# First layer: the loads of later weights and vector rows are asked for over steps 0 to 7 instead of all in step 0

## The chip, the cores and the metric

The kernel runs on one core of one Trainium2 chip. The metric is the device time of one execution in microseconds, the median of several runs. The kernel before takes 1694.06 us (three runs: 1685.83, 1694.06 and 1694.51).

## What is computed

Four layers follow each other on x, 64 sequences of 64 tokens with 128 features, with a context of the same shape. All is float32. The change lies in the first layer, an attention with relative positions and 16 heads of 64:

```python
kv = jnp.concatenate([memory, layer_input], axis=1)        # 128 keys for 64 queries
q = (layer_input @ Wq).reshape(b, q_len, n_head, d_head)
k = (kv @ Wk).reshape(b, kl, n_head, d_head)
v = (kv @ Wv).reshape(b, kl, n_head, d_head)
r = (pe @ Wr).reshape(kl, n_head, d_head)
ac = jnp.einsum('bqhd,bkhd->bhqk', q + content_bias, k)
bd = rel_shift(jnp.einsum('bqhd,khd->bhqk', q + position_bias, r))
scores = (ac + bd) * (1.0 / np.sqrt(d_head))
scores = jnp.where(slf_attn_mask[:, None, :, :], jnp.float32(-1000000000.0), scores)
attn = jax.nn.softmax(scores, axis=-1)
ctx = jnp.einsum('bhqk,bkhd->bqhd', attn, v).reshape(b, q_len, n_head * d_head)
out = layer_norm(layer_input + ctx @ Wo, ln1_g, ln1_b)
h = jax.nn.relu(out @ W1 + b1)
out = layer_norm(out + (h @ W2 + b2), ln2_g, ln2_b)
```

The second layer is self and cross attention with a feed-forward part, the third a gated fusion with the context, the fourth again two attentions and a choice of two among eight experts for each token.

## The kernel before

The 4096 tokens are cut into eight groups of eight sequences (512 tokens). In the first layer the sixteen heads are taken in eight pairs, so that there are 64 units, one for each group and pair of heads. `first_layer` runs them as a software pipeline that is written out by hand: one loop over steps t from -5 to 63 (line 605), in which each step holds work of several units. With `order["on"]` (line 1422) every engine keeps the order in which the first layer's instructions are written; the other layers are ordered by a scheduler when the program is built.

What a step t does, in the order of the code:

- `weights_turned` (line 536): the softmax weights of unit t are transposed on PE (`pt<-ident,s` in the profile) and copied out by DVE.
- `soft` (line 501): the scores of unit t+2 on PE (`psc`); DVE adds the relative part `skew` and takes the negated maximum `nm`; ACT takes eight exponentials (`s<-s,nm`).
- `keys` (line 468): the keys of unit t+3 on PE (`psk`), copied out by ACT as `kT`.
- `products` (line 547): weights times values of unit t (`av`), copied out by DVE.
- `values` (line 481): values for unit t+2 (`psv`), copied out half by ACT, half by DVE.
- `rel` (line 427): for unit t+5 the queries on PE (`proj<-kv,wq`), which DVE and ACT copy out as `qp` and `qc`; then the relative part (`pbd`), which DVE and ACT copy into `stage`. The shift of the relative part is made by way of DRAM: SP writes `stage` to `scr`, and when that has landed reads it back in two halves as `skew`.
- The output projection of unit t is added to `acc` on PE.
- `masked` (line 462): POOL adds the mask to a `skew` that was read back two steps before or so (`skew<-skew,mb`). `divided`: DVE takes the reciprocals of the sums `sm`, POOL multiplies.

In the steps -1, 7, 15 and so on SP loads the inputs of the next group (`kv`, 512 KB, and its mask, 64 KB) ahead of its `scr`. PSUM tiles of all these products come from one pool of seven banks (line 106). Transfers are issued by SP and ACT only here, each in the order of its queue; on ACT they stand among its arithmetic instructions.

The loads that the change touches stand in `later`, called at the end of step 0 (line 646), all on ACT's queue: `rows`, 22 vectors of 128 and one of 8, spread to all 128 partitions (a tile of 128x2824, 1412 KB); the feed-forward weights `w1_0` and `w2_0` of the first layer (256 KB each; `w` in the profile); `bd_small` and `wo1` (24 and 128 KB; `bd_small` and `wo`), from which `block_diagonal` makes weights of the second layer from step 12 on. The first five vectors of `rows` are those of the first layer and are read by `close` (line 563), which finishes a group and begins at the end of that group's last step, the first at step 7; the others are read by later layers. `later` also fills `pad` on POOL. From step 3 on each step sends a piece of `pad`, 325 KB, on ACT's queue to the DRAM buffer `hrows` (`empty_rows`, line 257), for the experts of the last layer.

Of the kernel before, what the change touches and what calls it, by code (L numbers as in the profile page):

```python
# [16 lines left out]
P = 128  # L17
B = 64
S = 64
D = 128  # L20
# [38 lines left out]
NROW = _RB + NE  # L59
# [35 lines left out]
def kernel(ctx: ExitStack, tc: tile.TileContext, a: dict, out: bass.AP):  # L95
    order = {"on": False}
    nc = Ordered(tc, order)
# [11 lines left out]
    def ctile(shape, name, dtype=F32):  # L109
        return const.tile(shape, dtype, tag=name, name=name)  # L110

    def wtile(shape, tag, bufs, dtype=F32):
        if tag in COMMON:
            return pools["common"].tile(shape, dtype, tag=tag, bufs=COMMON[tag], name=tag)
        return pools["work"].tile(shape, dtype, tag=tag, bufs=bufs, name=tag)
# [79 lines left out]
    rows = ctile([P, NROW], "rows")  # L195
# [10 lines left out]
    bd_small = ctile([P, 6, 8], "bd_small")  # L206
    qk1 = ctile([P, 2, D], "qk1")
    wo1 = ctile([P, 2, D], "wo1")
# [161 lines left out]
    def first_layer():  # L370
# [6 lines left out]
        w1_0 = wtile([P, 512], "w1", 1)  # L377
        w2_0 = wtile([P, NFC, D], "w2", 1)
# [34 lines left out]
        def mask_bias(g):  # L413
            nc.gpsimd.tensor_scalar(groups[g]["maskb"], groups[g]["m8"], NEG, None, ALU.mult)
# [5 lines left out]
        for h in range(2):  # L420
            pr = pmm("pr")
            for k in range(4):
                ks = slice(k * P, (k + 1) * P)
# [38 lines left out]
        def masked(sk, maskb):  # L462
            for r in range(2):
                nc.gpsimd.tensor_tensor(
                    sk[:, 4 * r : 4 * r + 4, :], sk[:, 4 * r : 4 * r + 4, :], maskb, ALU.add
                )

        def keys(p, kv):
            kT = wtile([P, NB, P], "kT0", 3)
            for hb in range(2):  # L470
                hs = slice(4 * hb, 4 * hb + 4)
                psk = pmm("psk")
                nc.tensor.matmul(
                    psk, lhsT=wk0[:, p * P : (p + 1) * P],
                    rhs=kv[:, hs, :, :].rearrange("p b c i -> p (b c i)"),
                    start=True, stop=True,
                )
                nc.scalar.copy(kT[:, hs, :], v3(psk[:, :], 4))
            return kT
# [21 lines left out]
        def soft(qc, kT, sk):  # L501
            psc2 = [pmm("psc") for _ in range(2)]
            for b in range(NB):
                for r in range(2):
                    rp = slice(64 * r, 64 * r + 64)
                    bp = slice(64 * (b % 2), 64 * (b % 2) + 64)
                    nc.tensor.matmul(
                        psc2[r][bp, (b // 2) * P : (b // 2 + 1) * P],
                        lhsT=qc[rp, b * S : (b + 1) * S],
                        rhs=kT[rp, b, :],  # L510
                        start=True,
                        stop=True,
                    )
            out = []
            for r in range(2):
                s = wtile([P, NBLK, P], "s", 6)
                nm = wtile([P, NBLK], "nm", 6)
                sm = wtile([P, NBLK], "sm", 6)
                nc.vector.tensor_tensor(s, v3(psc2[r][:, :], 4), sk[:, 4 * r : 4 * r + 4, :], ALU.add)
                nc.vector.tensor_reduce(nm, s, axis=AX.X, op=ALU.max, negate=True)  # L520
                for k in range(NBLK):
                    nc.scalar.activation(
                        s[:, k, :], s[:, k, :], AF.Exp,
                        bias=nm[:, k : k + 1], accum_out=sm[:, k : k + 1],
                    )
                out.append((s, sm))
            return out

        def divided(out):
            for s, sm in out:  # L530
                nc.vector.reciprocal(sm, sm)
            for s, sm in out:
                nc.gpsimd.tensor_tensor(s, s, last(sm[:, :], P), ALU.mult)
            return [s for s, sm in out]

        def weights_turned(ss):
            pTs = []
            for r in range(2):
                pt = pmm("pt0")
                for k in range(NBLK):  # L540
                    nc.tensor.transpose(pt[:, k * P : (k + 1) * P], ss[r][:, k, :], ident)
                pT = wtile([P, T], "pT", 4)
                nc.vector.tensor_copy(pT, pt)
                pTs.append(pT)
            return pTs

        def products(pTs, v, odd):
            av = pmm("av0")
            for b in range(NB):
                for r in range(2):  # L550
                    rp = slice(64 * r, 64 * r + 64)
                    nc.tensor.matmul(
                        av[rp, b * S : (b + 1) * S],
                        lhsT=v[:, b, odd, rp],
                        rhs=pTs[r][:, b * S : (b + 1) * S],
                        start=True,
                        stop=True,
                    )
            cx = wtile([P, T], "cx", 2)
            nc.vector.tensor_copy(cx, av)  # L560
            return cx
# [22 lines left out]

        pad = wtile([P, PADS, ROWW], "pad", 1)

        def later():
            nc.scalar.dma_start(rows, a["rows"].to_broadcast([P, NROW]))
            nc.scalar.dma_start(w1_0, a["w1_0"])
            nc.scalar.dma_start(w2_0, a["w2_0"].rearrange("(f c) d -> c f d", c=P))  # L590
            nc.scalar.dma_start(bd_small, a["bd"])
            nc.scalar.dma_start(wo1, a["wo1"])
            padi = wtile([P, PADS], "padi", 1, I32)
            nc.gpsimd.iota(padi, pattern=[[0, PADS]], base=2 * B * S, channel_multiplier=1)
            nc.gpsimd.memset(pad, 0.0)
            nc.gpsimd.tensor_copy(pad[:, :, D : D + 1].rearrange("p k c -> p (k c)"), padi)
            nc.gpsimd.memset(pad[:, :, D + 1 : D + 2], -1.0)
# [7 lines left out]
        for t in range(-REL, n):  # L605
            live = t >= 0
            if live:
                pTs = weights_turned(held[t]["s"])
            if 0 <= t + SOFT < n:
                h = held[t + SOFT]  # L610
                h["s"] = soft(h["qc"], h["k"], h["sk"])
            if 0 <= t + KEY < n:
                g, p = divmod(t + KEY, NP)
                held[t + KEY]["k"] = keys(p, groups[g]["kv"])
            if live:
                cx = products(pTs, vs[t // 2], t % 2)
            if 0 <= t + VAL < n:
                k = (t + VAL) // 2
                g, p = divmod(2 * k, NP)
                if t % 2 == 0:  # L620
                    vs[k] = wtile([P, NB, 2, P], "v0", 2)
                values(p, groups[g]["kv"], vs[k], t % 2)
            if t + REL < n:
                g, p = divmod(t + REL, NP)
                if p == 4 and g + 1 < NG:
                    load(g + 1)
                if p == 7 and g + 1 < NG:
                    mask_bias(g + 1)
                front = rel(p, groups[g])
                next(front)  # L630
            if live:
                g, p = divmod(t, NP)
                if p == 0:
                    acc = pools["psa"].tile([P, T], F32, tag="acc", name="acc")
                nc.tensor.matmul(acc, lhsT=wo0[:, p, :], rhs=cx, start=(p == 0), stop=(p == NP - 1))
                del held[t]
            if len(fresh) == 2 or t + REL >= n and fresh:
                masked(*fresh.pop(0))
            if 0 <= t + SOFT < n:
                held[t + SOFT]["s"] = divided(h["s"])  # L640
            if t + REL < n:
                qc, sk, maskb = next(front)
                held[t + REL] = {"qc": qc, "sk": sk}
                fresh.append((sk, maskb))
            if t == 0:
                later()
            if t == 12:
                folds = block_diagonal()
            if t >= 12:
                next(folds, None)  # L650
            if t > 2:
                empty_rows(t - 3, pad)
            if t > n - 12:
                empty_rows(t + 8, pad)
            if t == -REL:
                mask_bias(0)
            for e in list(ends):
                if next(e[1], "end") == "end":
                    ends.remove(e)
            if live and p == NP - 1:  # L660
                zT = wtile([P, T], "o", 2)
                nc.vector.tensor_tensor(
                    v3(zT[:, :], NB), v3(acc[:, :], NB), groups[g]["kv"][:, :, 1, :], ALU.add
                )
                ends.append((g, close(g, zT)))
# [860 lines left out]
```

## Time and profile before

| what | value |
|---|---|
| median of three runs | 1694.06 us |
| the profiled execution, on the device | 1692.51 us |
| its span in the profile | 1690.5 us |
| busy: PE, DVE, ACT, POOL | 92%, 69%, 59%, 53% |
| mean granted clock of PE | 0.943 |
| DMA packets' bytes over the span | 136.74 MB, mean 81 GB/s |
| queue of SP (q1), queue of ACT (q10) | 90.99 MB, 34.40 MB |
| `rows` load | one transfer, 1412 KB, issued at 50.1 us |

In the profile every instruction of the kernel has the line L74, that of the helper that records it, so groups are told apart by their tiles (`out<-in`). PE is TensorE's matmul row, PEld its weight loads; ACTq and SPq are the issuing of transfers on those two queues. In a timeline each row has the start, the time taken, the engine, the operation with its tiles, the count of merged instructions, and in brackets how long the engine had been idle before and what ended that. In a table of windows each engine has its busy time and, in brackets, its instructions; after them stand the clock that was granted to PE, the mean busy share of the 16 DMA engines, and GB/s. In a list of waits each row names who waited for whom, the sum in us, how often, and the longest.

### The profile page before, as it was taken

The numbers are of one execution on the slowest core, as the hardware profiler recorded it, in microseconds if no ns is written. First come the engines' busy times: TensorE is split into PE (matmuls) and PEld (weight loads), VectorE is DVE, ScalarE is ACT, GpSimd is POOL, SyncE is SP. The second block draws the span as 40 slices with busy tenths as digits, with TensorE's granted clock in tenths as the row PEclk, the third lists the DMA queues.
The fourth block names the chain that finished last, engine by engine and source line by source line (L and its number), as shares of the span: only waits on it lengthen the run. The fifth ranks groups of instructions, "written<-read, shape, count | busy, mean of one in ns | idle before, by whom it ended". The sixth has DMA issues, their size and how long they took to land. (4 is left out here: it accounts for less than half of the span.)

```text
span 1690.5 us, 45408 instructions
## 1 busy us (share of the span) xinstructions
PE 1548.2 (92%) x17588; PEld 1155.6 (68%) x17588; DVE 1161.5 (69%) x3147; ACT 1002.6 (59%) x2744; POOL 903.5 (53%) x867
## 2 busy tenths in 40 slices
PE   7799999999999999978888999989988998859995
PEld 4466666667666666646766776666767776759995
DVE  4477686777777677758887787677766677555554
ACT  4456556555555555535775655466767786427774
POOL 2445455555556464657886766653422234467543
PEclk9899999999999999979999999889998998759998
DMA  6756554555555555541000100000000000013243
GB/s 165 156 145 147 133 146 121 139 133 134 131 147 133 130 138 143 140 143 28 12 18 27 27 20 20 8 14 2 2 8 14 15 2 27 25 55 88 68 124 109
DMA packets 218356, 136.74 MB, mean 81 GB/s; under 512 B 38904, under 2 KB 202882, under 8 KB 218016
## 3 DMA queue, kind: packets, MB, share of 16 engines
q1 hardware_dynamic: 187024, 90.99, 23.1%
q10 hardware_dynamic: 26576, 34.40, 6.2%
q0 software_dynamic: 4544, 8.47, 1.6%
q8 instruction: 140, 2.29, 0.6%
q14 instruction: 72, 0.59, 0.1%
HBM read 66.95 MB, written 67.78 MB: 80 GB/s over the span
## 5 line engine op out<-in xcount | busy, mean ns | idle before, releaser
L74 ACT ACTIVATE s<-s,nm 128x128 f32<-128x128 f32 x512 | 198.1, 388 | 249.1 <-DVE nm L74 225.8
L74 POOL TENSOR_TENSOR s<-s,sm 128x512 f32<-128x512 f32 x128 | 130.4, 1039 | 251.8 <-DVE sm L74 251.8
L74 PE MATMUL pt<-ident,s 128*128 128x128 f32 x1536 | 216.3, 285 | 26.0 <-ACT kT L74 10.6
L74 POOL TENSOR_TENSOR s<-s,mx 128x512 f32<-128x512 f32 x160 | 164.3, 1046 | 99.1 <-DVE mx L74 92.9
L74 PEld LDWEIGHTS pt<-ident,s 128*128 128x128 f32 x1536 | 179.9, 146 | 46.4 <-issue 17.7
L74 ACT ACTIVATE pT<-pt 128x512 f32<-128x512 f32 x256 | 141.0, 601 | 78.1 <-PE pt L74 69.6
L74 POOL TENSOR_TENSOR skew<-skew,mb 128x512 f32<-128x512 f32 x128 | 159.9, 1271 | 40.3 <-DMA skew<-scr 39.6
L74 POOL TENSOR_TENSOR rs<-rs,nhalf 128x4 f32<-128x4 f32 x80 | 81.5, 1019 | 186.1 <-DVE rs L74 157.0
L74 PEld LDWEIGHTS av<-vb,pT 128*64 128x64 f32 x4096 | 134.1, 144 | 22.2 <-issue 13.2
L74 PE MATMUL av<-vb,pT 128*64 128x18 f32 x4096 | 142.3, 217 | 5.3 <-DVE o L74 4.8
L74 DVE TENSOR_REDUCE mx<-s 128x8 f32<-128x512 f32 x160 | 103.0, 677 | 44.4 <-ACT s L74 44.4
L74 PE MATMUL psk<-kv,wk 128*128 128x512 f32 x256 | 127.9, 622 | 0.0
L74 PE MATMUL psv<-wv,kv 128*128 128x256 f32 x512 | 127.4, 392 | 0.0
L74 PE MATMUL sc<-km,qs 32*64 32x256 f32 x2048 | 105.4, 422 | 9.4 <-ACT qs L74 5.4
L74 POOL DMA_INDIRECT yrows<-km,tob x78 | 77.3, 991 | 58.6 <-DVE tob L74 29.7
L74 DVE COPY pT<-pt 128x512 f32<-128x512 f32 x128 | 82.2, 683 | 37.3 <-PE pt L74 37.3
L74 PEld LDWEIGHTS pbd<-rT,qp 64*128 64x128 f32 x1024 | 63.0, 189 | 58.6 <-DVE qp L74 56.9
L74 PEld LDWEIGHTS psv<-wv,kv 128*128 128x128 f32 x512 | 92.2, 189 | 15.1 <-issue 1.0
L74 PEld LDWEIGHTS av<-pT,v 128*64 128x64 f32 x2048 | 66.5, 138 | 50.7 <-issue 29.0
L74 DVE TENSOR_TENSOR s<-sc,mb 128x512 f32<-128x512 f32 x128 | 82.5, 682 | 26.7 <-PE sc L74 26.7
L74 DVE TENSOR_TENSOR s<-psc,skew 128x512 f32<-128x512 f32 x128 | 87.5, 684 | 14.2 <-issue 6.3
L74 ACT ACTIVATION_READ_ACCUMULATOR s<-s,nm 128x1 f32 x512 | 95.6, 187 | 0.0
(231 smaller groups left out, 3564.0 us busy)
## 6 DMA issues: line engine op xcount, KB each, us to landing
scr<-stage SPq DMA_DIRECT2D x64, 516.0 KB
skew<-scr SPq DMA_DIRECT2D x128, 256.0 KB
hrows<-pad ACTq DMA_DIRECT2D x66, 325.0 KB
ctx<-in_ctxT SPq DMA_DIRECT2D x24, 256.0 KB
km<-hrows SPq DMA_DIRECT2D x78, 65.0 KB
fcw<-in_fc ACTq DMA_DIRECT2D x16, 256.0 KB
kv<-in_xT SPq DMA_DIRECT2D x8, 256.0 KB
kv<-in_ctxT SPq DMA_DIRECT2D x8, 256.0 KB
```

The source lines that it names most:

```text
L74: ins = it(*args, **kw)
```

## The change

`later` takes the step as an argument and is called in steps 0 to 7; each call issues a part of what one call issued before. `rows` is loaded in five pieces: its first five vectors in step 0, then four, four, four vectors and the rest (648 elements a partition) in steps 4 to 7. `w1_0` is loaded in step 1, `w2_0` in step 2, `bd_small` and `wo1` in step 3. All stay on ACT's queue, at the same place within a step. The work on POOL that fills `pad` moves into a function of its own and is called in step 0 as before.

```diff
-        def later():
-            nc.scalar.dma_start(rows, a["rows"].to_broadcast([P, NROW]))
-            nc.scalar.dma_start(w1_0, a["w1_0"])
-            nc.scalar.dma_start(w2_0, a["w2_0"].rearrange("(f c) d -> c f d", c=P))
-            nc.scalar.dma_start(bd_small, a["bd"])
-            nc.scalar.dma_start(wo1, a["wo1"])
+        def later(t):
+
+            if t == 0:
+                nc.scalar.dma_start(rows[:, 0 : 5 * D], a["rows"][:, 0 : 5 * D].to_broadcast([P, 5 * D]))
+            elif t == 1:
+                nc.scalar.dma_start(w1_0, a["w1_0"])
+            elif t == 2:
+                nc.scalar.dma_start(w2_0, a["w2_0"].rearrange("(f c) d -> c f d", c=P))
+            elif t == 3:
+                nc.scalar.dma_start(bd_small, a["bd"])
+                nc.scalar.dma_start(wo1, a["wo1"])
+            elif t < 8:
+                lo, hi = (5 + (NROW - 5 * D) * k // (4 * D) for k in (t - 4, t - 3))
+                ks = slice(lo * D, NROW if t == 7 else hi * D)
+                nc.scalar.dma_start(rows[:, ks], a["rows"][:, ks].to_broadcast([P, ks.stop - ks.start]))
+
+        def pads():
             padi = wtile([P, PADS], "padi", 1, I32)
...
             if t == 0:
-                later()
+                pads()
+            if 0 <= t < 8:
+                later(t)
```

## The prediction

> **What bounds the kernel now.** I read the page first: PE is busy 92% of the span, and in its row of 40 slices the first two stand at 7, the next fifteen at 9. So the first layer (up to about 712 us) goes at PE's pace, and only a hole in PE's row can be won back. The change sits in step 0, so next I cut the first 200 us into windows of 20 us.
>
> ```profile
> core 0: us, PE busy (x) PEld busy (x) DVE busy (x) ACT busy (x) POOL busy (x), PEclk, DMA share, GB/s
> 40.00:60.00 20.00, 20.00 (x213) 13.45 (x212) 13.43 (x22) 7.68 (x25) 9.91 (x12) 1.00 0.98 200
> 60.00:80.00 20.00, 9.43 (x85) 6.34 (x84) 5.73 (x11) 10.11 (x40) 8.51 (x7) 0.74 0.57 133
> 80.00:100.00 20.00, 20.00 (x210) 13.34 (x209) 13.98 (x25) 11.15 (x42) 9.03 (x8) 1.00 0.42 119
> ```
>
> PE is full before and after, and works 9.43 of 20 us between 60 and 80, at a granted clock of 0.74. Just ahead of the hole the DMA engines are full (0.98). Third, the timeline of 40 to 90 us, to see what stands at both ends of the hole.
>
> ```profile
> 50.09 0.34 ACTq L74 DMA_DIRECT2D rows<-in_rows  x1
> 51.91 6.47 ACTq L74 DMA_DIRECT2D w<-in_w  x2
> 57.97 2.08 SPq L74 DMA_DIRECT2D skew<-scr  x2
> 59.72 0.66 PE L74 MATMUL pt<-ident,s 128*128 128x128 f32 x4
> 65.75 0.33 ACTq L74 DMA_DIRECT2D bd_small<-in_bd  x1
> 66.71 0.33 ACTq L74 DMA_DIRECT2D wo<-in_wo  x1
> 66.83 2.48 POOL L74 TENSOR_TENSOR skew<-skew,mb 128x512 f32<-128x512 f32 x2 [11.63 <-DMA skew<-scr]
> 67.15 0.40 ACT L74 ACTIVATE s<-s,nm 128x128 f32<-128x128 f32 x1 [16.50 <-DMA skew<-scr]
> 70.24 1.04 ACT L74 COPY kT<-psk 128x512 f32<-128x512 f32 x2
> 70.94 1.09 PE L74 MATMUL pt<-ident,s 128*128 128x128 f32 x4 [10.57 <-ACT kT L74]
> ```
>
> ACT does no arithmetic for 16.50 us, from 50.65 to 67.15, and in that time its queue issues just the five transfers of `later`. They stand in one queue with ACT's arithmetic, so ACT cannot pass them. Why they take so long follows from the built program's list of waits: all transfers of SP and ACT take eight semaphores in turn, and an issue waits until the transfer eight places earlier has landed. The second `w` waits for the scr of step -1, `bd_small` and `wo` for its two skews. The times agree: the second `w` goes out at 58.4 us, when the skews, which wait for the same scr, go out (57.97), and the last two when the skews have landed (POOL starts on them at 66.83). PE then lacks a PSUM bank: its pt waits for ACT's kT copy, which has stood behind the issues. The waits of 45 to 85 us say the same in totals:
>
> ```profile
> ACT s L74 <- DMA skew<-scr: 16.5, 1, 16.5
> POOL skew L74 <- DMA skew<-scr: 15.1, 2, 11.6
> PE pt L74 <- ACT kT L74: 10.6, 1, 10.6
> ```
>
> Last, what it costs. Each step has one proj on PE, so its starts are the step's clock (46.92 is step 0):
>
> ```profile
> 46.92 1.02 PE L74 MATMUL proj<-kv,wq 128*128 128x512 f32 x2
> 56.76 1.02 PE L74 MATMUL proj<-kv,wq 128*128 128x512 f32 x2
> 79.66 1.02 PE L74 MATMUL proj<-kv,wq 128*128 128x512 f32 x2
> 89.50 1.02 PE L74 MATMUL proj<-kv,wq 128*128 128x512 f32 x2
> ```
>
> Steps 1 and 3 take 9.84 us, step 2 takes 22.90. Lost: **13.06 us**, of which 10.57 is the idle time and 2.49 PE at half clock afterwards (granted clock 0.50 from 66 to 74 us; psk 2.94 us where it otherwise takes 1.98, psc 1.98 for 1.10).
>
> **The change, part by part.** The order of instructions on PE, DVE, POOL and SP is the same in both programs; on ACT alone transfers move, and four are added.
>
> *Removed: the hold of ACT in step 0.* One issue stays there, a rows piece of 128x640 elements, 320 KB in place of 1412. Its semaphore's earlier transfer, a skew of step -2, has landed by 49.70. ACT's next work, the exponentials of s, then starts when nm is ready, at about 53.5 (DVE's nm of that step 52.84 + 0.69), instead of 67.15. The kT copies follow 3.1 us later (70.24 - 67.15), at 56.6, ahead of PE's pt at 59.72. PE's 10.57 us go, and with them the slow clock: -13.06.
>
> *What is late next.* The skews of step -1 are used by DVE in step 2. The hole has hidden them. Their scr is issued at 49.20, behind the loads of kv and the mask. The nearest row for such a load with about 320 KB beside it is step 7, where a pad of 325 KB goes out: scr issued 132.68, skews 139.51, 6.83 us. That gives scr landed at 56.0, against 57.97 now; the skews took 5.14 us in step -2 (44.56 to POOL's start at 49.70), so 61.2; POOL's first half 1.27 (skew with mask, median 1269 ns): 62.4. DVE wants it one step after the 52.11 of step 1, at 61.95: half a microsecond late. PE feels that only at its next proj (66.6), which needs a bank that DVE frees, so the cover is 4.6 us and the cost 0. If the scr were no faster than now and the skews took the 8.9 us of now (57.97 to 66.83), DVE would be 6.1 us late and PE would lose 6.1 - 4.6 = 1.5, perhaps 3 with what trails behind. Bounds 0 to 3; I take 0, since the 1412 KB that filled the DMA engines are cut to 320.
>
> *Moved and added: steps 1 to 7.* ACT issues w1, w2, bd_small with wo1, then four rows pieces (three of 256 KB, one of 324). Each is 0.33 us in ACT's queue; four more are 1.3 us in all, and ACT waits for DVE's nm once a step (55.7 us in 15 waits between 85 and 250 us, 3.7 each). Cost 0. Their semaphore waits in the new program go to transfers of the step before or earlier. The latest are the skews of two steps before, for wo1 and a pad in step 3, a rows piece in step 4, pads in steps 5 and 6. In step 2 of the present run proj starts at 79.66, the skews go out at 88.31 at the end of scr's 83.47, and some 5 us later (93.4) they have landed; ACT's slot two steps on would be about 79.66 + 19.7 + 3.7 = 103. Cover 9.6 us, cost 0.
>
> *The DMA engines.* A step of today's steady kind moves 516 (scr) + 512 (skews) + 325 (pad) = 1353 KB in 9.84 us, 137 GB/s; between 40 and 60 us they moved 200. A piece adds 256 KB, 26 GB/s. Does that lengthen SP's chain of scr, landing, skew?
>
> ```profile
> 93.31 0.36 SPq L74 DMA_DIRECT2D scr<-stage  x1
> 98.61 1.25 SPq L74 DMA_DIRECT2D skew<-scr  x2
> 103.16 0.37 SPq L74 DMA_DIRECT2D scr<-stage  x1
> 132.68 0.48 SPq L74 DMA_DIRECT2D scr<-stage  x1
> 139.51 1.26 SPq L74 DMA_DIRECT2D skew<-scr  x2
> ```
>
> With a pad an scr takes 5.30 us, with a load of 576 KB more 6.83, so 256 KB cost at most 1.5. After the skews SP is done at 99.86 and waits to 103.16: 3.3 us of cover. Only step 7, with load and piece together, comes near its end (139.51 + 1.26 = 140.77, next scr 142.52: 1.75 of cover). Cost 0; bounds 0 to 4 (four pieces, 1 each, if the cover were gone).
>
> *Later readers.* The first five rows are read at 163.8 us, w1 at 181.9, bd_small at 194.2, the other rows from 742.7; the last piece goes out near 120. Nothing to pay.
>
> The rule that speaks against the change is in the Trainium skill, "DMA: Bandwidth & Descriptors", section "Rules for kernel authors": coalesce many small transfers, and use 1 MiB or more per transfer for bandwidth. Going by it, with the about 2 us of fixed cost that the page gives, four more transfers would cost an estimated 8 us and the sum would be -5; no run here shows that figure for ACT's queue.
>
> **Sum.** 13.06 - 0 = 13.06 us. The span goes from 1690.5 to 1677.4, the profiled execution (1692.51) to 1679.5. That execution lies 1.5 under the median of 1694.06, inside the runs' 1685.83 to 1694.51; I forecast **1680**.
>
> **The rivals.**
> *A, the skews of step -1 stay late.* For it: POOL's 11.63 us wait is as much due to SP's backlog (scr issued at 49.20 for stage copies that ended near 42) as to rows. Price 1.5 to 3: 1682.5.
> *B, splitting costs.* One wait for a landing for each added transfer. The nearest row is cols, issued at 0.73 and used at 3.11: 2.4 us, times four 9.5, leaving 3.5: 1689. Against it: none of these landings has a reader before 163.8. This is the coalescing rule above in the kernel's own rows.
> *C, given back later,* by the DMA engines, which used the hole to catch up (1.02 in the 2 us from 70), or in the next layer's start: 4 to 13 us, 1684 to 1692. Against it: each engine has the same order, and steps 3 to 6 run at 9.84 with PE full at a DMA share of 0.55.
> *D, slower.* The holds return, several times: in steps 3 to 6 ACT again waits for skews before it can compute. If SP's chain is more than 9.6 us behind at such a step, ACT stands, PE runs out of banks, and each hold is worth the one measured here, 13.06. Two of them make +13: 1705. Against it: the lag estimated above is half a microsecond at step 2 and shrinks.
>
> **Chances.** Forecast 0.72, A 0.12, B 0.04, C 0.08, D 0.04. A measurement of this kernel tells about 0.5% from no change, 8.5 us here. Forecast and A lie beyond that unless the runs' own spread (8.7 us) takes some: faster 0.79. B, most of C and what the spread takes: same 0.16. D and a little of C: slower 0.05. The forecast's own range is 1674 to 1685; with A, B and half of C it reaches 1689.
>
> **What would show it.** Right: a 128x640 rows issue near 50.1 and ACT's exponentials at 53 to 54; proj at 66.6 and 76.4; PE full and the clock 1.00 from 60 to 80; POOL's wait for that skew about 6 us, not 11.6; ACT's issues each under 1 us in steps 1 to 7. Wrong: proj of step 2 later than 68 (A); a wait of PE or POOL over 2 us between 80 and 130 (C, D); ACT idle behind an issue for more than 4 us (D); the first layer shorter by 13 us and the span not (C).

## The result, and the profile after

The changed kernel takes 1680.7 us (median of 20 runs, 1672.83 to 1688.36); the kernel before takes 1690.97 us (median of 20 runs). The ratio is 0.9941, with a 95% interval of 0.9929 to 0.9953: 10.0 us shorter, between 8.0 and 12.0. The profiled execution took 1672.83 us with a span of 1670.9, the shortest of its runs; so in what follows stretches of the trace are compared, not the two spans.

The windows of the changed kernel over the stretch that held the hole:

```profile
40.00:60.00 20.00, 20.00 (x210) 13.31 (x209) 13.86 (x25) 11.68 (x42) 10.29 (x14) 1.00 0.85 161
60.00:80.00 20.00, 20.00 (x211) 13.21 (x209) 14.47 (x26) 11.68 (x42) 13.38 (x12) 1.00 0.70 150
80.00:100.00 20.00, 20.00 (x210) 13.16 (x208) 13.97 (x26) 11.85 (x43) 8.99 (x8) 1.00 0.71 152
```

PE is full and its clock whole in all three. The DMA engines are less full between 40 and 60 (0.85 for 0.98) and fuller after 80 (0.71 for 0.42): the loads are spread. The timeline of the changed kernel shows why PE is full:

```profile
46.38 0.49 SPq L74 DMA_DIRECT2D scr<-stage  x1
47.20 0.34 ACTq L74 DMA_DIRECT2D rows<-in_rows  x1
50.73 0.40 ACT L74 ACTIVATE s<-s,nm 128x128 f32<-128x128 f32 x1 [2.97 <-DVE nm L74]
53.21 1.26 SPq L74 DMA_DIRECT2D skew<-scr  x2
57.04 0.33 ACTq L74 DMA_DIRECT2D w<-in_w  x1
58.40 2.49 POOL L74 TENSOR_TENSOR skew<-skew,mb 128x512 f32<-128x512 f32 x2 [6.04 <-DMA skew<-scr]
66.88 0.39 ACTq L74 DMA_DIRECT2D w<-in_w  x1
```

(This execution reached step 0 some 3 us earlier, at 44.03 for 46.92. That has nothing to do with the change: a second execution of the changed kernel, below, reached it at 47.70.) ACT issues one transfer, and 3.53 us after it the exponentials begin, when DVE's `nm` is ready and not when a transfer has landed. SP's scr of step -1 takes 6.83 us until the skews can go out (46.38 to 53.21), 8.77 before. POOL still waits 6.04 us for the skews of step -1, where it waited 11.63. In the waits of 45 to 85 us PE has no row left, and ACT none over 4 us at a time:

```profile
POOL skew L74 <- DMA skew<-scr: 20.5, 5, 6.0
ACT s L74 <- DVE nm L74: 9.5, 3, 3.6
ACT s L74 <- DMA w<-in_w: 3.0, 1, 3.0
```

The 3.0 us behind a `w` name the issue that stood last in the queue; they are as long as the waits for `nm` around them. POOL's waits do not reach PE here, as the starts of proj show, one per step from step 0:

```profile
44.03 1.02 PE L74 MATMUL proj<-kv,wq 128*128 128x512 f32 x2
53.87 1.02 PE L74 MATMUL proj<-kv,wq 128*128 128x512 f32 x2
63.71 1.02 PE L74 MATMUL proj<-kv,wq 128*128 128x512 f32 x2
73.56 1.02 PE L74 MATMUL proj<-kv,wq 128*128 128x512 f32 x2
```

Every step takes 9.84 or 9.85. From step 0 to step 3 it is 29.53 us where it was 42.58.

### The profile page after: what moved, and what is told of

It reads as the page before. It is cut to its first block, busy times and chain, and to the rows that moved or that the text cites. A ratio compares the mean times of both kernels' runs of the same rounds, so it can differ in the third digit from the quotient of the medians.

```text
span 1670.9 us, 45410 instructions
## 1 busy us (share of the span) xinstructions
PE 1534.6 (92%) x17588; PEld 1147.1 (69%) x17588; DVE 1161.2 (70%) x3147; ACT 1001.9 (60%) x2744; POOL 903.9 (54%) x867
## 4 chain that ended last, share of the span: by engine, by line
PE 63%; DVE 18%; POOL 6%; ACT 6%; DMA 3%; issue 3%; SPq 0%; DVEq 0%; POOLq 0%; ACTq 0%
PE av L74 8%; PE psv L74 8%; PE proj L74 7%; PE psk L74 6%; PE pt L74 6%; PE f L74 5%; DVE mx L74 4%; PE pbd L74 4%; PE tok L74 4%; DVE s L74 4%; PE psc L74 4%; PE acc L74 3%; PE tr L74 3%; ACT z L74 2%; PE sc L74 2%
```

## The experiments

All distances below are between starts of proj. "Steps 0 to 3" is 29.52 us when PE is full.

**The volume without the hold.** `rows` whole and w1 stay in step 0; the other loads move.

```diff
 if t == 0:
     nc.scalar.dma_start(rows, a["rows"].to_broadcast([P, NROW]))
+    nc.scalar.dma_start(w1_0, a["w1_0"])
 elif t == 2:
     nc.scalar.dma_start(w2_0, a["w2_0"].rearrange("(f c) d -> c f d", c=P))
 elif t == 3:
     nc.scalar.dma_start(bd_small, a["bd"])
     nc.scalar.dma_start(wo1, a["wo1"])
```

> Step 0 issues rows whole (1412 KB) and w1 (256 KB), 1668 of the 2076 KB; w2 goes to step 2, bd_small and wo1 to step 3. In this program neither issue of step 0 waits for scr or skew of step -1. Theory (the hole comes from ACT held behind issues that wait for a transfer still under way): ACT's exponentials start some 4 us after the rows issue, and from proj of step 0 to proj of step 3 it takes 29.5 us (PE full) to 32.5, against 42.6 before; the 0 to 3 us are the skews of step -1, which stay as late as before. Rival (the volume itself fills the DMA engines and delays the skews until PE starves): 1668/2076 of the 13.1 lost, so about 40.

Measured: steps 0 to 3 take 31.56 us (46.62 to 78.18), 2.0 lost; ACT's exponentials start 3.53 us after the rows issue. Ratio to before 0.9945, interval 0.9921 to 0.997. With 80% of the bytes still in step 0 most of the hole is gone. What remains is the late skew of step -1, in the timeline of this kernel:

```profile
64.26 2.49 POOL L74 TENSOR_TENSOR skew<-skew,mb 128x512 f32<-128x512 f32 x2 [10.40 <-DMA skew<-scr]
65.56 0.69 DVE L74 TENSOR_TENSOR s<-psc,skew 128x512 f32<-128x512 f32 x1 [4.16 <-POOL skew L74]
68.95 1.13 PE L74 MATMUL acc<-cx,wo 128*128 128x512 f32 x2 [1.51 <-DVE cx L74]
```

POOL gets the skew 14.5 us after the rows issue, in the changed kernel 11.2. DVE stands 4.16 us before its addition, and its copy `cx`, which is queued behind that addition, comes late for PE's `acc`. Of the 4.16 us PE loses 2.0, so 2.1 were covered.

**The hold without the volume.** The changed kernel, with step 0's 320 KB of `rows` cut into five transfers and `bd_small` and `wo1` issued behind them.

```diff
 if t == 0:
-    nc.scalar.dma_start(rows[:, 0 : 5 * D], a["rows"][:, 0 : 5 * D].to_broadcast([P, 5 * D]))
+    nc.scalar.dma_start(rows[:, 0 * D : 1 * D], a["rows"][:, 0 * D : 1 * D].to_broadcast([P, 1 * D]))
...
+    nc.scalar.dma_start(rows[:, 4 * D : 5 * D], a["rows"][:, 4 * D : 5 * D].to_broadcast([P, 1 * D]))
+    nc.scalar.dma_start(bd_small, a["bd"])
+    nc.scalar.dma_start(wo1, a["wo1"])
```

> As the changed kernel, but step 0 loads its first five rows vectors one by one (five of 64 KB) and also bd_small and wo1: 472 KB in seven issues. The last three wait, by the eight semaphores' turn, for scr and for the two skews of step -1, as in the kernel before. Theory (hold): ACT does no arithmetic from the first issue until the skews land, 11 us after it in the changed kernel; its exponentials are 8 us late, PE idles about 5 and then works at a lowered clock for a while: proj of step 0 to proj of step 3 takes 29.5 + 6 to 8 = 35.5 to 37.5 us. Rival (volume): 472/2076 of 13.1, 3 lost, so 32.5 or less.

Measured: steps 0 to 3 take 38.87 us (46.27 to 85.14), 9.35 lost, above the range of the hold and far above the rival's 3. Ratio 0.9984, interval 0.9965 to 1.0003. Its timeline:

```profile
49.44 5.68 ACTq L74 DMA_DIRECT2D rows<-in_rows  x5
60.24 0.34 ACTq L74 DMA_DIRECT2D bd_small<-in_bd  x1
61.33 0.34 ACTq L74 DMA_DIRECT2D wo<-in_wo  x1
61.77 0.40 ACT L74 ACTIVATE s<-s,nm 128x128 f32<-128x128 f32 x1 [11.77 <-DMA skew<-scr]
```

The last two issues, of 24 and 128 KB, go out when the skews of step -1 land, as in the kernel before, and ACT's arithmetic only then. The loss is 6.42 us of PE waiting for ACT's kT, more than the 5 expected, and 2.93 of slow clock, which the expectation had left loose. The windows of this kernel show the clock (the column after the five engines):

```profile
58.00:60.00 2.00, 1.14 (x16) 0.95 (x16) 0.00 (x0) 0.00 (x0) 0.00 (x0) 1.00 1.07 256
60.00:62.00 2.00, 0.00 (x0) 0.00 (x0) 0.00 (x0) 0.23 (x1) 0.55 (x1) 0.85 0.92 182
62.00:64.00 2.00, 0.00 (x0) 0.00 (x0) 0.18 (x1) 2.00 (x12) 2.00 (x3) 0.50 0.48 73
68.00:70.00 2.00, 2.00 (x29) 1.52 (x22) 0.71 (x2) 0.00 (x0) 0.36 (x1) 0.50 0.96 243
70.00:72.00 2.00, 2.00 (x4) 0.67 (x2) 1.93 (x4) 0.97 (x5) 2.00 (x2) 0.59 0.25 41
```

It falls to half at 61.4 and is back at 71.65 (by slices of 0.5 us; in the one from 61.0 to 61.5 its mean is 0.91). In the kernel before it was at half from 65.6 to 75.8, and in a second profile of that kernel, which is described further down, from 62.8 to 73.0. The first and the last slice of that stretch in the second profile, and the wait of PE in it:

```profile
62.00:63.00 1.00, 0.00 (x0) 0.00 (x0) 0.00 (x0) 0.00 (x0) 0.00 (x0) 0.90 1.15 298
73.00:74.00 1.00, 1.00 (x3) 0.52 (x4) 0.97 (x2) 0.00 (x0) 0.21 (x1) 0.98 1.17 276
69.79 1.08 PE L74 MATMUL pt<-ident,s 128*128 128x128 f32 x4 [10.62 <-ACT kT L74]
```

So the slow stretch lasted 10.2 us in all three, however long PE had been idle, and what it costs depends on how much of it is left when PE works again: 6.1, 4.9 and 3.2 us of it cost 2.93, 2.49 and 1.66. That is why 6.42 us of idle time cost more slow work than 10.57 did. The Trainium skill, "TensorE: Matmul & The Clock Gate", section "Part 1: The HAM clock gate (the "warmup" mystery)", says that an idle window of some 3.4 us halves PE's clock. Here the clock fell 2.3, 5.2 and 3.6 us after PE's last matmul, around that figure, and the next kernel, whose longest wait of PE there is 1.4 us, keeps a clock of 1.00.

**Only the two smallest loads moved.** The kernel before, with 152 of its 2076 KB in step 3.

```diff
 if t == 0:
     nc.scalar.dma_start(rows, a["rows"].to_broadcast([P, NROW]))
     nc.scalar.dma_start(w1_0, a["w1_0"])
     nc.scalar.dma_start(w2_0, a["w2_0"].rearrange("(f c) d -> c f d", c=P))
-    nc.scalar.dma_start(bd_small, a["bd"])
-    nc.scalar.dma_start(wo1, a["wo1"])
+elif t == 3:
+    nc.scalar.dma_start(bd_small, a["bd"])
+    nc.scalar.dma_start(wo1, a["wo1"])
```

> As the kernel before, with only bd_small and wo1 (152 of 2076 KB) moved to step 3. The last issue of step 0 is w2, which waits for scr of step -1 and no longer for its skews. Theory (hold): ACT is free when scr has landed, about 8.5 us after the rows issue in place of 17; its exponentials are 5 us late, of which 3 are covered: 2 to 4 us lost, so proj of step 0 to proj of step 3 takes 31.5 to 33.5 us. Rival (volume): nearly all of the loss stays, 12 of 13.1: about 41.6.

Measured: steps 0 to 3 take 32.66 us (46.97 to 79.63), 3.1 lost. Ratio 0.9953, interval 0.9931 to 0.9975. 7% of the bytes bring back three quarters of the hole. Its timeline shows ACT held for less than half as long, until the second `w` is out:

```profile
51.00 6.94 ACTq L74 DMA_DIRECT2D w<-in_w  x2
58.05 0.40 ACT L74 ACTIVATE s<-s,nm 128x128 f32<-128x128 f32 x1 [7.34 <-DMA rows<-in_rows]
```

PE's two waits there are 1.42 us for ACT's kT and 0.81 for DVE's `cx`, behind a skew that is late as in the first of these kernels.

**One large piece.** The changed kernel, with `rows` whole in step 4.

```diff
-if t == 0:
-    nc.scalar.dma_start(rows[:, 0 : 5 * D], a["rows"][:, 0 : 5 * D].to_broadcast([P, 5 * D]))
...
-elif t < 8:
...
+elif t == 4:
+    nc.scalar.dma_start(rows, a["rows"].to_broadcast([P, NROW]))
```

> As the changed kernel, but rows is loaded whole (1412 KB) in step 4 in place of five pieces. Theory: no issue waits for an unfinished transfer, so there is no hold; the load delays scr and skews of steps 4 and 5 by up to 7 us, and about 6.7 are covered (2.1 between POOL's part and DVE's need, 4.6 until PE needs the bank): 0 to 3 us lost between proj of step 4 and proj of step 8 (39.4 if PE is full), the time as that of the changed kernel or up to 3 us longer. The rule to coalesce transfers: not longer than the changed kernel, up to 8 us shorter. Rival (volume): a hole of 9 us in steps 5 and 6.

Measured: steps 0 to 3 take 29.53 us, steps 4 to 8 take 39.37, so nothing is lost; ratio 0.9922, interval 0.9899 to 0.9945. 1412 KB at once cost nothing in step 4, though they delay SP's chain:

```profile
90.42 0.88 SPq L74 DMA_DIRECT2D scr<-stage  x1
99.92 2.49 POOL L74 TENSOR_TENSOR skew<-skew,mb 128x512 f32<-128x512 f32 x2 [10.37 <-DMA skew<-scr]
101.21 0.69 DVE L74 TENSOR_TENSOR s<-psc,skew 128x512 f32<-128x512 f32 x1 [0.98 <-POOL skew L74]
101.99 1.25 SPq L74 DMA_DIRECT2D skew<-scr  x2
```

The scr of step 4 takes 11.57 us until its skews can go out, and POOL gets the skew of step 3 4.64 us after the proj of step 5. DVE waits 0.98 us for it and PE not at all. In step 0 the skew came 7.8 us after the proj of step 1 (56.46 to 64.26, with `rows` and w1 in step 0), and that cost 2.0. No issue holds ACT for long either: the longest, a pad behind `rows`, takes 1.28 us.

**Where the changed kernel falls short of 13.06.** Its steps 9 to 11 took 9.90 and 10.49 us where the kernel before has 9.84 and 9.84. Four more runs: the kernel before and the changed kernel once more, the one with `rows` whole in step 4 once more, and the changed kernel with its last piece a step later:

```diff
-            elif t < 8:
-                lo, hi = (5 + (NROW - 5 * D) * k // (4 * D) for k in (t - 4, t - 3))
-                ks = slice(lo * D, NROW if t == 7 else hi * D)
+            elif t < 7 or t == 8:
+                n = min(t - 4, 3)
+                lo, hi = (5 + (NROW - 5 * D) * k // (4 * D) for k in (n, n + 1))
+                ks = slice(lo * D, NROW if n == 3 else hi * D)
...
-            if 0 <= t < 8:
+            if 0 <= t < 9:
                 later(t)
```

> The kernel before, profiled once more. The changed kernel gained 12.4 us between the first layer's step 0 and its last proj in the one pair of profiles, and about 10 in the medians. If the hole has the same size in every execution, proj of step 0 to proj of step 3 takes 42.6 us again, and proj of step 0 to the last proj 637.6. If the first profile had a large hole by chance, 39 to 41 here.

> The changed kernel, profiled and timed once more. Steps 0 to 3 take 29.5 us again. If the 0.7 us that steps 9 to 11 lost in its first profile (10.27, 9.90, 10.49 where others take 10.28, 9.84, 9.84) come from the last rows piece beside the load of step 7, they are lost again; if by chance, not. Ratio to before 0.9925 (12.4 us) if the profiles tell the whole effect; 0.994 if 2 us of it are given back after the first layer.

> The changed kernel with its last rows piece (324 KB) in step 8 in place of step 7, in which SP also loads 576 KB. Theory (piece and load collide and make a skew late): steps 9 to 11 go at 10.28, 9.84, 9.84, the 0.7 us are back. Rival (four more transfers in eight semaphores' turn cost it, or chance): 10.27, 9.90, 10.49 as in the changed kernel, or the loss one step later.

> The kernel with rows loaded whole in step 4, timed beside the changed kernel. By the profiles it is 0.6 us shorter than the changed kernel (624.6 against 625.2 from proj of step 0 to the last proj): ratio to before 0.992, within 0.2% of the changed kernel. By the rule to coalesce transfers as the cause of its lower first median, 0.1 to 0.2% below the changed kernel.

| kernel | steps 0 to 3 | steps 3 to 12 | step 0 to last proj | from there to the end | span |
|---|---|---|---|---|---|
| before | 42.58 | 89.44 | 637.59 | 1006.0 | 1690.5 |
| before, again | 41.80 | 89.45 | 636.75 | 1007.1 | 1689.6 |
| changed | 29.53 | 90.15 | 625.17 | 1001.7 | 1670.9 |
| changed, again | 29.52 | 90.59 | 625.64 | 1010.1 | 1683.4 |
| last piece in step 8 | 29.67 | 89.45 | 624.63 | 1008.5 | 1678.6 |
| rows whole in step 4 | 29.53 | 89.45 | 624.56 | 1001.1 | 1671.7 |
| the same, again | 29.53 | 89.44 | 624.46 | 1001.7 | 1671.5 |

The loss of steps 9 to 11 is there in both profiles of the changed kernel (0.7 and 1.15 us) and gone, in the one profile of that kernel, when the last piece leaves step 7, in which SP loads 576 KB for the next group. (That kernel lost 0.15 us in step 2. Its skew of step -1 reached POOL 5.92 us after the proj of step 1, later than in the other kernels of the table without a hole, and DVE waited 2.3 us for it.) First the changed kernel, then the one with the piece in step 8; the proj rows are those of steps 9, 10 and 11:

```profile
133.04 1.02 PE L74 MATMUL proj<-kv,wq 128*128 128x512 f32 x2
136.27 2.50 POOL L74 TENSOR_TENSOR skew<-skew,mb 128x512 f32<-128x512 f32 x2 [7.28 <-DMA skew<-scr]
137.88 0.91 DVE L74 TENSOR_SCALAR rs<-mv 128x4 f32<-128x4 f32 x1
142.94 1.02 PE L74 MATMUL proj<-kv,wq 128*128 128x512 f32 x2
146.61 2.66 DVE L74 TENSOR_SCALAR z<-z,mv,rs 128x128 f32<-128x128 f32 x4
150.53 1.15 PE L74 MATMUL av<-pT,v 128*64 128x64 f32 x30 [0.21 <-DVE pT L74]
153.43 1.02 PE L74 MATMUL proj<-kv,wq 128*128 128x512 f32 x2
```

```profile
134.57 1.02 PE L74 MATMUL proj<-kv,wq 128*128 128x512 f32 x2
137.13 2.51 POOL L74 TENSOR_TENSOR skew<-skew,mb 128x512 f32<-128x512 f32 x2 [8.08 <-DMA skew<-scr]
139.42 0.25 DVE L74 TENSOR_SCALAR rs<-mv 128x4 f32<-128x4 f32 x1
144.42 1.02 PE L74 MATMUL proj<-kv,wq 128*128 128x512 f32 x2
148.08 1.89 DVE L74 TENSOR_SCALAR z<-z,mv,rs 128x128 f32<-128x128 f32 x4
154.26 1.02 PE L74 MATMUL proj<-kv,wq 128*128 128x512 f32 x2
```

The skew reaches POOL 3.23 us after proj in the one and 2.56 in the other; the one loses 0.7 us and the other nothing. DVE does not wait for that skew in either; what it lacks is time. In these steps it also finishes a group: `rs` and `z` belong to its layer norm. `rs` starts 4.84 or 4.85 us after proj in every kernel, and while POOL works on its 128x512 tiles it does not end before the POOL instruction under way does (138.79 and 138.77 here, 139.67 and 139.64 there, and so in all five profiles in which POOL is busy then); in the five in which POOL is idle it takes 0.17 us. The four `z` of the next step take 2.66 us here, 3.05 in the second profile of the changed kernel, and 1.26 in the kernel before. DVE copies the transposed weights `pT` behind them, and in both profiles of the changed kernel, and in no other of the table, PE's `av` waits for that copy. Why DVE is held beside POOL no run here shows.

Timed side by side the changed kernel came to 0.9937 of before (interval 0.9916 to 0.9957) and the one with `rows` whole in step 4 to 0.9931 (0.991 to 0.9952). From step 0 to the last proj the latter is 0.6 to 1.2 us shorter in the traces; the times do not tell the two apart.

## Why the prediction was right, step by step

- *The hole is ACT's hold, and the hold is the semaphores' turn.* Right. With 80% of the bytes and no hold 2.0 us were lost, with the hold and 472 KB 9.35, and taking off the last two issues gave back 9.9 of 13.06. That eight semaphores are taken in turn was read from the built program; the traces show that each held issue goes out when the transfer of its turn lands. The Trainium skill, "DMA: Bandwidth & Descriptors", section "Anatomy of one DMA — SWDGE (gpsimd) path", says that a wait on a semaphore takes place on the issuing sequencer, not in the DMA engines. The section is about transfers that GpSimd issues; for ACT's, the 11.77 and 16.50 us in which ACT stood agree.
- *-13.06.* The mechanism was right and the size a little large. The hole was 13.06 us in the first profile of the kernel before and 12.28 in the second, 12.7 on the mean. The idle time was the same, 10.57 and 10.62; the slow work after it, 2.49 in the sum, was 1.66 in the second, because the clock came back sooner after PE's start. In both profiles of the changed kernel the hole is gone to 0.01 us.
- *The skews of step -1.* Right: scr took 6.83 us as the row of step 7 had given, and POOL began 11.2 us after the rows issue (forecast 11.1). That scr met the row to the digit is luck; it took 7.17 in the second profile. Bounds 0 to 3 for skews that stay as late as before were met by the kernel that leaves the volume in step 0 (2.0). But PE's first wait there was `acc`, for a copy of DVE's behind the late addition, and not the bank of proj that I had named as the cover's end. So the cover was 2.1 us and not 4.6; it did not matter, because DVE was only 0.9 us late.
- *ACT's added issues, and their semaphore waits.* Right: 0.33 to 0.44 us each. One pad behind a rows piece, in step 4, took 1.69 us where I had said under 1; the time that ACT waits for `nm` took it in. Another sign of being wrong, a wait of POOL over 2 us between 80 and 130, came true (up to 5.84 us) and meant nothing: the kernel before has such waits there too, up to 5.8 us, and PE had none in either.
- *The DMA engines beside step 7.* "Cost 0; bounds 0 to 4" was the one term put too low. I had named step 7 as the place, with 1.75 us of cover taken from a trace in which the hole had given SP's chain time to catch up: there the scr of step 7 goes out 3.8 us after its proj, in the changed kernel 11.1. Without that time 0.7 and 1.15 us are lost; the kernel with the hold in step 0 has the same pieces, in step 7 too, and loses nothing there (9.85 and 9.84). The price of a piece, "at most 1.5", was also too low for one of them: the scr of steps 4 to 6 took 0.9, 1.5 and 2.8 us more than that of step 3 (7.83, 8.42 and 9.66 for 6.90). And the way to PE was another: no late skew was waited for, but POOL's late additions held up DVE's `rs` and `z`. (The 137 GB/s of that part count a KB as 1000 bytes, while its sizes are in units of 1024; it is 141.)
- *The sum.* 12.7 - 0.9 = 11.8 us by the traces (637.2 against 625.4 on the mean), inside the measured 8.0 to 12.0. That the forecast of 1680 came within 0.7 us of the median is luck in part: it started from an execution of 1692.51 us, 1.5 above the median of the 20 runs, and took off 3 us more than the change brought. From 1690.97 the same sum gives 1677.9.
- *The rivals.* A (skews stay late), C (given back) and D (holds return) did not come about, but for the 0.9 us of step 7. B and the rule to coalesce: the one large piece costs nothing and five pieces cost 0.9 us on the mean, because one of them met a load; a fixed price for each added transfer would show in steps 4 to 6 as well, and they go at 9.84 us. The about 2 us that the prediction took from the Trainium skill are, in its "DMA: Bandwidth & Descriptors", section "Anatomy of one DMA — SWDGE (gpsimd) path", a fit for transfers that GpSimd issues; these are ACT's.
- *After the first layer* nothing can be shown as gained or lost: see the last section.

## What to carry to other kernels

A transfer issued from an engine that also computes can stop that engine's arithmetic, and here its size decided little (2.0 of 13.06 us): ask which earlier transfer its semaphore must see landed, and how many issues stand in a row. A few loads in a burst reach back to transfers still under way, the same loads one a step reach back to finished ones. When a hole is taken out, take the cover of the neighbouring steps again without it: the idle time had let slower chains catch up. And cover that holds in one step need not hold in another: the skew that came 4.64 us after proj cost nothing in step 5, one that came 3.23 us after it cost 0.7 in step 9, where DVE has more to do.

## What was not expected

From the last proj of the first layer to the end the same instructions took between 1001.1 and 1010.1 us in these executions, and the two profiles of one kernel, the changed one, differ by 8.4. The 100 us that begin 400 us after that proj, in its first and its second profile:

```profile
1069.20:1169.20 100.00, 90.80 (x1010) 64.95 (x1011) 76.55 (x218) 60.70 (x123) 46.96 (x40) 0.94 0.02 7
```

```profile
1073.34:1173.34 100.00, 91.07 (x968) 64.73 (x967) 67.93 (x189) 58.84 (x120) 46.54 (x39) 0.88 0.02 7
```

With a granted clock of 0.94 PE gets through 1010 matmuls, with 0.88 through 968, while it is busy for the same time. In the first layer, wherever PE does not pause, the same steps repeat to about 0.02 us. Of the 12.5 us between the two spans 8.4 arise behind the last proj, 3.7 ahead of step 0 and 0.5 between. So most of this spread arises in the later layers. Their clock differs from one execution to the next; whether it is the cause or follows from PE's pauses there is not shown. An effect of 1 us in the first layer can be read from the trace and not from the times.
